# A graph network on one NeuronCore: the list scheduler's ranking of begun products, its view of the port that VectorE and GpSimd share, and the last two groups worked in halves

## The chip, the cores and the metric

The kernel runs on one core of a Trainium2 chip. The metric is the device time of one launch in microseconds, from three runs. Besides those times there is one execution taken by the hardware profiler. Engine names are those of the profile: PE is TensorE, PEld its weight loads, DVE is VectorE, ACT is ScalarE, POOL is GpSimd, SP is SyncE, which issues most of the DMAs.

## The reference, cut to what matters

The input x holds 128 graphs of 64 nodes with 256 features, all in 32-bit floats, and one 64 x 64 adjacency matrix serves all graphs. Four layers follow one another. Each normalises x over its features, takes the positive part, and adds its result to x:

```python
h = jnp.maximum(_layernorm(x, axis=-1), 0.0); x = x + _L0_gnn_ref(h, adj, ...)   # adj products, then LSTMs
h = jnp.maximum(_layernorm(x, axis=-1), 0.0); x = x + _L1_gnn_ref(h, adj, adj, ...)  # Laplacian, attention, MLP
h = jnp.maximum(_layernorm(x, axis=-1), 0.0); x = x + _L2_gnn_ref(h, adj, ...)   # graph attention
h = jnp.maximum(_layernorm(x, axis=-1), 0.0); x = x + _L3_gnn_ref(h, adj, ...)   # spectral filter
```

- Layer 0 multiplies by the adjacency and by a weight matrix, twice, and then runs four LSTMs (windows of 1, 2, 3 and 4 nodes) one after another over the result.
- Layer 1 takes a product with the scaled Laplacian, a normalisation, attention with four heads under a mask, a normalisation, a two-layer network with GELU, and a normalisation.
- Layer 2 is graph attention: two scores for each node, their sum for each pair of nodes, a leaky ReLU, a mask, a softmax over the nodes, and the product of the weights with the features and a matrix W.
- Layer 3 needs the eigenvectors U of a 64 x 64 matrix made from the adjacency. It computes `U @ (relu(U.T @ h @ W1 + b1) @ W2 + b2)`.

## The kernel before, in words

**Tiling.** Two graphs make a tile of 128 rows (partitions), so there are 64 tiles. Layer 0 is worked in 8 groups of 8 tiles. Its results are stored to DRAM, and layers 1 to 3 are worked in 16 groups of 4 tiles (`HT = 4`): a group is fetched, goes through `layer1`, `layer2` and `layer3`, and is stored two tiles at a time. A buffer of the kind "big" holds 4 tiles x 256 features. A product over the nodes of a graph (`mix`) uses 64 x 64 pieces of the PE array, four at a time. Such a series is recorded as one indivisible operation, a "burst". All other products use the whole array. In the profile every matrix product of 32-bit floats shows as two records.

**A planner writes the order.** No engine's order is written by hand. The code records every operation with `Plan.record` (line 114 on): its engine, what it depends on, the buffers that it needs. `Plan.schedule` then plays the program through on assumed costs and decides, for each engine, in which order the operations are issued and which buffer each gets. `Plan.issue` (line 341) emits them in that order, so every instruction has line 347 in the profile. [...] The assumed times decide the order alone; the chip's own durations decide when things happen.

**How the planner chooses.** For each engine it takes the operation that can start first. Among those that can start now, it takes the one with the smallest rank. Three things matter here:

- `rank` (line 331). For groups of layer 0 it sorts by group, then by the order of recording. For groups of layers 1 to 3 it sorts by group, and within that by `6 * max(op.group - g, 0) - op.path`, where `path` is the longest chain of assumed times to the program's end. The last six groups count as one group (`self.ends`), so they are run down together. Bursts are kept together by a flag ahead of the rank, since a change between 64 x 64 pieces and the whole array is charged 0.178 us. The eigenvector computation (the group `EIG`, "aside") is first on PE and GpSimd and last elsewhere.
- The port. `op.port` (line 162) marks all GpSimd operations, and VectorE operations whose operands are all in SBUF. The planner lets only one of them run at a time: after one is placed, `port = t + cost` (line 295) bars the others until its assumed end.
- PSUM. There are eight banks of 512 floats. Six are of the kind "bank" from the start. Two of the kind "seed" serve layer 0's LSTMs, and join the others when layer 0 is done. A value gets its bank when its first product is placed, and the bank comes free after its last reader.

**Costs.** `Plan.cost` (line 179) gives GpSimd `0.44 + 0.14 * n` for a power and `0.12 + 0.00218 * n` for anything else with n elements in a row. A DMA from SP is charged its transfer time and 2.2 us of latency.

**The last layers.** `ln_stats` computes means and variances of 4 tiles on VectorE, then four small GpSimd operations on 128 x 4 elements (one of them a power) make scale and shift. `relu_norm` (line 1609) applies them on ScalarE, a tile at a time. `mix_fm` (line 1616) is a burst followed by two copies out of PSUM by ScalarE. `layer2` (line 1698) and `layer3` (line 1732) work on all 4 tiles of a group in each step: every step of layer 3, for instance, waits until the step before has done all four tiles.

Of the kernel before, what the change touches and what calls it, by code (L numbers as in the profile page):

```python
# [8 lines left out]
ALU = mybir.AluOpType  # L9
# [3 lines left out]
N = 64  # L13
# [55 lines left out]
class Plan:  # L69
# [44 lines left out]
    def record(self, eng, name, args, kw):  # L114
        op = self.run
        if op is None:
            op = Op(eng, name, args, kw, self.group)
            op.lead = self.lead
            if self.behind:
                op.deps.add(self.behind)  # L120
        else:
            op.calls.append((name, args, kw))
        aps = [(a, i == 0) for i, a in enumerate(args) if self.is_ap(a)]
        aps += [(a, k in ("out", "accum_out")) for k, a in kw.items() if self.is_ap(a)]
        for a, write in aps:
            ap = a.ap if isinstance(a, Virt) else a
            if str(ap.space) == "DRAM" and not self.tc.is_my_tile(ap.tensor):
                continue
            key = ap.tensor.name
            if isinstance(a, Virt):  # L130
                key = id(a.val)
                op.vals[a.val] = True
            step, count = ap.ap[0]
            p0, f0 = (ap.offset // step, ap.offset % step) if step else (0, ap.offset)
            ends = [s * (n - 1) for s, n in ap.ap[1:]]
            region = (p0, p0 + count, f0 + sum(min(e, 0) for e in ends), f0 + sum(max(e, 0) for e in ends) + 1)
            if isinstance(a, Virt) and a.val.kind in ("bank", "seed"):
                op.deps |= {o for o in a.val.users if o.eng != eng}
                a.val.users.append(op)
            reads, writes = self.seen.setdefault(key, ([], []))  # L140
            for log in (reads, writes) if write else (writes,):
                for r, o in log:
                    if o is not op and r[0] < region[1] and region[0] < r[1] and r[2] < region[3] and region[2] < r[3]:
                        op.deps.add(o)
                        if log is writes:
                            op.late.add(o)
                if write:
                    log[:] = [(r, o) for r, o in log if not (
                        region[0] <= r[0] and r[1] <= region[1] and region[2] <= r[2] and r[3] <= region[3])]
            (writes if write else reads).append((region, op))  # L150
        if eng == "PE":

            val = args[0].val
            if val.last and val.last is not op:
                op.deps.add(val.last)
            val.last = op
        if op is self.run:
            return self.link(op)
        flat = [a.ap if isinstance(a, Virt) else a for a, _ in aps]
        op.cost, op.lat = self.cost(op, flat)  # L160

        op.port = eng == "G" or (eng == "V" and not name.startswith("bn_") and "reduce" not in name
                                 and all(str(ap.space) == "SB" for ap in flat))
        op.index = len(self.ops)
        self.ops.append(op)
        self.link(op)
        if self.whole:
            self.run = op
# [10 lines left out]
    def cost(op, aps):  # L179
# [37 lines left out]
                c += 0.12  # L217
            return c, c + 0.15
        if op.eng == "G":
            c = 0.44 + 0.14 * n if op.kw.get("op") is ALU.pow else 0.12 + 0.00218 * n  # L220
            return c, c + 0.05
        c = max(0.6, free(aps[0]) * aps[0].ap[0][1] * 4e-6 / 0.39)
        return c, c + 2.2
# [6 lines left out]
    def schedule(self):  # L230
# [20 lines left out]
        while len(order) < len(self.ops):  # L251
# [40 lines left out]
                many, cost, lat = op.many, cost + 0.178, lat + 0.178  # L292
            now[e] = t + cost
            if op.port:
                port = t + cost
            end = t + lat
            for v in op.vals:
                if v.buf is None:
# [10 lines left out]
            for o in op.after:  # L309
                o.wait -= 1  # L310
                if o.eng != e:
                    o.ready = max(o.ready, end + self.slack(o))
                else:
                    o.ready = max(o.ready, end - 0.01 if op in o.late and e != "PE" else t + cost)
                if not o.wait:
                    ready[o.eng].append(o)
# [14 lines left out]
    def rank(self, op):  # L331
        if op.group == self.aside:
            return (-2 if op.eng in ("PE", "G") else 1000, op.index)
        if op.eng == "SP":
            return (op.group, 0, op.index)
        g = min(max(op.group - op.lead, 0), self.ends)
        if op.group < REST:
            return (g, -op.lead, op.index)
        return (g, 6 * max(op.group - g, 0) - op.path, op.index)

    def issue(self):
        real = lambda a: a.real() if isinstance(a, Virt) else a
# [551 lines left out]
P = 128  # L894
# [116 lines left out]
def gnn_kernel(ctx: ExitStack, tc: tile.TileContext, a, out):  # L1011
# [54 lines left out]
    def bank(name):  # L1066
        return plan.value("bank")
# [201 lines left out]
    def tm(n=HT, f=D):  # L1269

        return plan.value("big")[:, :n * f].rearrange("p (t f) -> p t f", f=f)
# [334 lines left out]
        V.reduce_max(mx, s, axis=AX.X)  # L1606
        V.tensor_sub(s, s, mx.unsqueeze(2).to_broadcast(list(s.shape)))

    def relu_norm(x):
        sc, bi = ln_stats(x)  # L1610
        h = tm()
        for t in range(HT):
            ACT.activation(h[:, t, :], x[:, t, :], AF.Relu, scale=sc(t), bias=bi(t))
        return h

    def mix_fm(h, m):

        dst = fm()
        for i, ps in enumerate(mix(lambda t, c: h[:, t, tok(c)], m, HT)):
            evac(dst.rearrange("p c (t b n) -> p c t b n", t=HT, b=2)[:, :, :, i, :], ps, 1)  # L1620
        return dst

    def layer1(x):
# [71 lines left out]
            V.tensor_mul(x2[:, t0:t0 + 2, :], x2[:, t0:t0 + 2, :], vec(g3, 2))  # L1695
            V.tensor_add(x[:, t0:t0 + 2, :], x[:, t0:t0 + 2, :], x2[:, t0:t0 + 2, :])

    def layer2(x):


        h = relu_norm(x)
        big, stat = plan.value("big"), plan.value("stat")
        s12 = stat[:, 2 * HT:4 * HT].rearrange("p (k t) -> p k t", k=2)
        for k in range(2):
            for t in range(HT):
                V.scalar_tensor_tensor(big[:, t * D:(t + 1) * D], h[:, t, :], 1.0, wa[:, k, :], op0=ALU.mult, op1=ALU.mult, accum_out=s12[:, k, t:t + 1])

        s2d, s1m, e2, e = (big[:, i * HT * N:(i + 1) * HT * N].rearrange("p (t n) -> p t n", n=N) for i in range(4))
        V.tensor_mul(s2d, vec(ident2), s12[:, 1, :].unsqueeze(2).to_broadcast([P, HT, N]))
        G.tensor_add(s1m, vec(mask2), s12[:, 0, :].unsqueeze(2).to_broadcast([P, HT, N]))  # L1710
        ps = bank("s2")[:, :HT * N]
        PE.matmul(ps, same, flat(s2d), start=True, stop=True)
        V.tensor_add(flat(e), ps, flat(s1m))
        V.tensor_scalar(e2, e, 0.2, None, op0=ALU.mult)
        V.tensor_max(e, e, e2)
        softmax_shift(e, stat[:, :HT])
        attn = plan.value("attn").rearrange("p (t k) -> p t k", t=HT)
        for i in range(2):
            r = half(i)
            ACT.activation(attn[r, :, r], e[r], AF.Exp)  # L1720
        ssum = stat[:, HT:2 * HT]
        V.reduce_sum(ssum, attn, axis=AX.X)
        V.reciprocal(ssum, ssum)
        pT = plan.value("big")[:, :HT * P]
        evac(pT, transposes([attn[:, t, :] for t in range(HT)]), 1)
        aT = mix_fm(h, lambda t: pT[:, tok(t)])
        for t0 in (0, 2):
            ps = proj_tm(lambda c, t: aT[:, c, tok(t)], W2a, 2, t0)
            for t in (t0, t0 + 1):
                V.scalar_tensor_tensor(x[:, t, :], ps[:, (t - t0) * D:(t - t0 + 1) * D], ssum[:, t:t + 1], x[:, t, :], op0=ALU.mult, op1=ALU.add)  # L1730

    def layer3(x):
        h = relu_norm(x)
        for t0 in (0, 2):
            G.tensor_add(x[:, t0:t0 + 2, :], x[:, t0:t0 + 2, :], vec(b3b, 2))
        aT = mix_fm(h, lambda t: Ub)
        hid = tm(HT, P)
        ps = bank("hid")
        for t in range(HT):
            for c in range(2):  # L1740
                PE.matmul(ps[:, tok(t)], aT[:, c, tok(t)], W3a[:, c, :], start=c == 0, stop=c == 1)
        V.tensor_tensor(hid, ps.rearrange("p (t f) -> p t f", t=HT), vec(nb3a), op=ALU.max)
        uT = tm(HT, P)
        for i, ps in enumerate(mix(lambda t, c: hid[:, t, :], lambda t: UTb, HT, 1)):
            V.tensor_tensor(uT.rearrange("p t (b n) -> p t b n", b=2)[:, :, i, :], ps[:, 0], vec(C3[:, half(i)]), op=ALU.add)
        for t0 in (0, 2):
            ps = proj_tm(lambda c, t: uT[:, t, :], W3b.unsqueeze(1), 1, t0)
            V.tensor_add(pair(x, t0), ps, pair(x, t0))

    for g in range(NT // HT):  # L1750
        plan.group = REST + g
        x = fetch(put[g // 2][:, g % 2 * HT:(g % 2 + 1) * HT])
        layer1(x)
        layer2(x)
        layer3(x)
        for t0 in range(0, HT, 2):
            SP.dma_start(xout[g][:, t0:t0 + 2, :], x[:, t0:t0 + 2, :])
    plan.issue()
# [53 lines left out]
```

## Time and profile before

| | |
|---|---|
| runs, median (lowest to highest) | 2116.32 us (2113.99 to 2117.18) |
| the profiled execution's own time | 2117.02 us |
| its span, first to last instruction | 2115.2 us |
| instructions | 48093 |
| PE, DVE, ACT, POOL busy | 2072.3, 1767.0, 1094.7, 756.6 us |
| groups of layer 0 and the eigenvectors | about 0 to 1270 us |
| groups of layers 1 to 3 | about 1270 us to the end |

The profile is read from whole to part: the busy time of each engine over the span; then the same by stretches of time, which shows where PE, the busiest, is idle; then PE's waits and the chain of waits in the stretch where it is idle most; then single instructions there. A line of such a view names the engine, the operation, what it writes and reads (buffer numbers left out, so `big<-bank,Whh` is a buffer of the kind big, written from a PSUM bank and from a constant that lives in the memory once used for Whh), the shape as partitions x elements, and how many were merged.

### The profile page before, as it was taken

The numbers are of one execution on the slowest core, as the hardware profiler recorded it, in microseconds if no ns is written. First come the engines' busy times: TensorE is split into PE (matmuls) and PEld (weight loads), VectorE is DVE, ScalarE is ACT, GpSimd is POOL, SyncE is SP. The second block draws the span as 40 slices with busy tenths as digits, with TensorE's granted clock in tenths as the row PEclk, the third lists the DMA queues.
The fourth block names the chain that finished last, engine by engine and source line by source line (L and its number), as shares of the span: only waits on it lengthen the run. The fifth ranks groups of instructions, "written<-read, shape, count | busy, mean of one in ns | idle before, by whom it ended". The sixth has DMA issues, their size and how long they took to land.

```text
span 2115.2 us, 48093 instructions
## 1 busy us (share of the span) xinstructions
PE 2072.3 (98%) x17924; PEld 1675.9 (79%) x17924; DVE 1767.0 (84%) x6669; ACT 1094.7 (52%) x2451; POOL 756.6 (36%) x1144
## 2 busy tenths in 40 slices
PE   8999999999999999999999999999999999999997
PEld 6688689688788788788788789877778778877775
DVE  7788888889999999999988956868779699885785
ACT  3344544534543543543444345666666567575763
POOL 6522212222201201201100215685467658663452
PEclk9999999999999999999999999999999999999999
DMA  6000100100100100100000211100000000000001
GB/s 229 1 3 13 52 3 2 62 2 2 60 1 1 61 1 2 46 1 10 32 1 21 90 49 35 62 1 22 22 21 22 21 22 22 22 2 11 1 12 51
DMA packets 44875, 57.83 MB, mean 27 GB/s; under 512 B 8929, under 2 KB 38497, under 8 KB 44641
## 3 DMA queue, kind: packets, MB, share of 16 engines
q1 hardware_dynamic: 43536, 53.71, 7.9%
q8 instruction: 141, 2.31, 0.5%
q10 hardware_dynamic: 1104, 1.05, 0.2%
q14 instruction: 94, 0.76, 0.1%
HBM read 37.53 MB, written 16.78 MB: 26 GB/s over the span
## 4 chain that ended last, share of the span: by engine, by line
PE 80%; DVE 13%; issue 2%; ACT 2%; POOL 2%; DMA 0%; SPq 0%; ACTq 0%; DVEq 0%; POOLq 0%
PE bank L347 64%; PE seed L347 16%; DVE arena L347 5%; DVE big L347 4%; DVE stat L347 2%; ACT mids L347 1%; DVE mids L347 1%; POOL stat L347 1%; DVE sums L347 1%; POOL big L347 1%; ACT big L347 0%; DMA arena<-put 0%; DVE bank L347 0%; POOL sums L347 0%; DVE seed L347 0%
## 5 line engine op out<-in xcount | busy, mean ns | idle before, releaser
L347 PE MATMUL bank<-big,Wih 128*128 128x512 f32 (+4 forms) x1802 | 554.5, 424 | 2.9 <-DVE big L347 1.9
L347 PEld LDWEIGHTS bank<-big,Wih 128*128 128x128 f32 x1802 | 314.7, 190 | 145.5 <-issue 95.5
L347 PE MATMUL bank<-big,sums 128*128 128x128 f32 (+3 forms) x2328 | 375.7, 289 | 5.2 <-DVE seed L347 2.5
L347 ACT ACTIVATE mids<-bank,bl 128x512 f32<-128x512 f32 (+2 forms) x432 | 247.2, 576 | 214.3 <-PE bank L347 195.2
L347 PEld LDWEIGHTS bank<-big,sums 128*128 128x128 f32 (+1 forms) x2328 | 298.5, 180 | 42.8 <-issue 19.6
L347 PE MATMUL bank<-big,Whh 128*128 128x128 f32 (+3 forms) x1294 | 312.3, 327 | 0.0
L347 DVE TENSOR_TENSOR arena<-arena 64x42 f32<-64x42 f32 (+6 forms) x1358 | 276.5, 231 | 18.4 <-POOL arena L347 1.2
L347 PEld LDWEIGHTS bank<-big,Whh 128*128 128x128 f32 x1294 | 214.0, 191 | 18.5 <-issue 10.5
L347 ACT ACTIVATE mids<-seed,bl 128x256 f32<-128x256 f32 (+2 forms) x192 | 102.0, 531 | 217.0 <-PE seed L347 209.0
L347 DVE TENSOR_TENSOR big<-mids 128x512 f32<-128x512 f32 (+2 forms) x256 | 151.1, 597 | 27.1 <-ACT mids L347 17.1
L347 POOL TENSOR_SCALAR stat<-stat 128x4 f32<-128x4 f32 (+1 forms) x228 | 68.4, 301 | 281.1 <-DVE stat L347 268.9
L347 PE MATMUL seed<-big,sums 128*128 128x128 f32 (+3 forms) x896 | 143.3, 291 | 0.0
L347 DVE SCALAR_TENSOR_TENSOR arena<-arena 64x1 f32<-64x1 f32 (+15 forms) x565 | 136.1, 264 | 4.5 <-POOL arena L347 1.0
L347 POOL TENSOR_TENSOR big<-big 128x128 f32<-128x128 f32 (+2 forms) x55 | 32.9, 600 | 294.6 <-DVE big L347 151.7
L347 POOL TENSOR_TENSOR stat<-stat,mhalf 128x4 f32<-128x4 f32 (+1 forms) x114 | 123.9, 1087 | 4.8
L347 ACT COPY seed<-bank 128x128 f32<-128x128 f32 (+2 forms) x192 | 54.0, 281 | 135.8 <-PE bank L347 128.5
L347 ACT ACTIVATE mids<-big 128x256 f32<-128x256 f32 (+2 forms) x176 | 89.5, 511 | 66.3 <-DVE big L347 62.1
L347 ACT COPY mids<-bank 128x256 f32<-128x256 f32 (+3 forms) x290 | 94.8, 352 | 51.9 <-PE bank L347 51.5
L347 PEld LDWEIGHTS seed<-big,sums 128*128 128x128 f32 (+1 forms) x896 | 118.4, 183 | 3.5 <-issue 0.3
L347 DVE TENSOR_SCALAR arena<-arena 64x1 f32<-64x1 f32 (+10 forms) x506 | 100.4, 206 | 7.8 <-POOL arena L347 0.5
L347 DVE TENSOR_TENSOR big<-big,mids 128x256 f32<-128x256 f32 (+2 forms) x196 | 99.0, 509 | 7.0 <-ACT mids L347 6.0
L347 PE MATMUL bank<-Wih,big 128*128 128x256 f32 x408 | 104.8, 383 | 0.0
(517 smaller groups left out, 4480.4 us busy)
## 6 DMA issues: line engine op xcount, KB each, us to landing
big<-in_x_dram SPq DMA_DIRECT2D x29, 512.0 KB, 5.0
put<-big SPq DMA_DIRECT2D x15, 512.0 KB, 3.2
big<-put SPq DMA_DIRECT2D x8, 512.0 KB, 6.4
out_dram<-big SPq DMA_DIRECT2D x16, 256.0 KB, 2.6
Wih<-in_WihT_dram SPq DMA_DIRECT2D x3, 1024.0 KB, 11.4
Whh<-in_WhhT_dram SPq DMA_DIRECT2D x3, 1024.0 KB, 12.9
arena<-put SPq DMA_DIRECT2D x3, 512.0 KB, 5.9
sums<-put SPq DMA_DIRECT2D x3, 512.0 KB, 4.3
```

The costliest lines, as they stand in the source:

```text
L347: getattr(self.engines[op.eng], name)(*map(real, args), **{k: real(a) for k, a in kw.items()})
```

## The change

Six edits. Five are in the planner, and change no operation, only the order and the choice of buffers:

1. `begun(op)` is true for a PE operation one of whose PSUM values already has its bank. In groups of layer 0 such an operation gets group 0 in its rank, so it comes ahead of operations of all groups that have not begun a bank. In groups of layers 1 to 3 it gains 6 us of path.
2. `op.hold`: an operation all of whose operands have two dimensions and at most 64 elements in a row bars the port for at most 0.06 us instead of its whole cost. This holds for GpSimd and for VectorE.
3. A GpSimd operation other than a power, with at most 64 elements, is charged 0.2 us (for 4 elements it was 0.129).
4. What depends on a DMA from SP and runs on another engine is taken to be ready 1.5 us later than before.
5. For this, `relu_norm` and `mix_fm` take a range of tiles.

The sixth changes operations: `layer2` and `layer3` take a `step`. It is 4 tiles for groups 0 to 13, and 2 tiles for the last two groups. Every step of both layers, with its statistics, softmax, bursts and copies, is then recorded once for tiles 0 and 1 and once for tiles 2 and 3, and neither half waits for the other. The diff, cut:

```diff
@@ record
+        wide = max(ap.ap[-1][1] if len(ap.ap) == 2 else 65 for ap in flat) > 64
+        op.hold = op.cost if wide else 0.06
@@ cost
-            c = 0.44 + 0.14 * n if op.kw.get("op") is ALU.pow else 0.12 + 0.00218 * n
+            c = 0.44 + 0.14 * n if op.kw.get("op") is ALU.pow else 0.12 + 0.00218 * n if n > 64 else 0.2
@@ schedule
             if op.port:
-                port = t + cost
+                port = t + min(cost, op.hold)
...
                 if o.eng != e:
-                    o.ready = max(o.ready, end + self.slack(o))
+                    o.ready = max(o.ready, end + self.slack(o) + (1.5 if e == "SP" else 0.0))
@@ rank
         if op.group < REST:
-            return (g, -op.lead, op.index)
-        return (g, 6 * max(op.group - g, 0) - op.path, op.index)
+            return (0 if self.begun(op) else g, -op.lead, op.index)
+        return (g, 6 * max(op.group - g, 0) - op.path - (6 if self.begun(op) else 0.0), op.index)
+
+    def begun(self, op):
+
+        return op.eng == "PE" and any(v.kind in ("bank", "seed") and v.buf is not None for v in op.vals)
@@ helpers
-    def relu_norm(x):
-        sc, bi = ln_stats(x)
-        h = tm()
-        for t in range(HT):
-            ACT.activation(h[:, t, :], x[:, t, :], AF.Relu, scale=sc(t), bias=bi(t))
+    def relu_norm(x, h=None, t0=0, n=HT):
+        h = tm() if h is None else h
+        sc, bi = ln_stats(x[:, t0:t0 + n], n)
+        for t in range(n):
+            ACT.activation(h[:, t0 + t, :], x[:, t0 + t, :], AF.Relu, scale=sc(t), bias=bi(t))
         return h
-    def mix_fm(h, m):
-
-        dst = fm()
-        for i, ps in enumerate(mix(lambda t, c: h[:, t, tok(c)], m, HT)):
-            evac(dst.rearrange("p c (t b n) -> p c t b n", t=HT, b=2)[:, :, :, i, :], ps, 1)
+    def mix_fm(h, m, dst=None, t0=0, n=HT):
+
+        dst = fm() if dst is None else dst
+        part = dst[:, :, t0 * P:(t0 + n) * P].rearrange("p c (t b n) -> p c t b n", t=n, b=2)
+        for i, ps in enumerate(mix(lambda t, c: h[:, t0 + t, tok(c)], lambda t: m(t0 + t), n)):
+            evac(part[:, :, :, i, :], ps, 1)
         return dst
@@ layers 2 and 3
+    def layer2(x, step):
+
+        h, big, attn = tm(), plan.value("big"), plan.value("attn").rearrange("p (t k) -> p t k", t=HT)
+        pT, aT = plan.value("big")[:, :HT * P], fm()
+        for t0 in range(0, HT, step):
+            n, ts = step, slice(t0, t0 + step)
+            relu_norm(x, h, t0, n)
+            stat = plan.value("stat")
...
+            mix_fm(h, lambda t: pT[:, tok(t)], aT, t0, n)
...
+    def layer3(x, step):
+        h, aT, hid, uT = tm(), fm(), tm(HT, P), tm(HT, P)
+        for t0 in range(0, HT, step):
+            n, ts = step, slice(t0, t0 + step)
+            relu_norm(x, h, t0, n)
+            for u0 in range(t0, t0 + n, 2):
+                G.tensor_add(x[:, u0:u0 + 2, :], x[:, u0:u0 + 2, :], vec(b3b, 2))
+            mix_fm(h, lambda t: Ub, aT, t0, n)
...
+            V.tensor_tensor(hid[:, ts], ps[:, :n * P].rearrange("p (t f) -> p t f", t=n), vec(nb3a, n), op=ALU.max)
+            for i, ps in enumerate(mix(lambda t, c: hid[:, t0 + t, :], lambda t: UTb, n, 1)):
+                V.tensor_tensor(uT[:, ts].rearrange("p t (b n) -> p t b n", b=2)[:, :, i, :], ps[:, 0], vec(C3[:, half(i)], n), op=ALU.add)
+            for u0 in range(t0, t0 + n, 2):
+                ps = proj_tm(lambda c, t: uT[:, t, :], W3b.unsqueeze(1), 1, u0)
+                V.tensor_add(pair(x, u0), ps, pair(x, u0))
...
         layer1(x)
-        layer2(x)
-        layer3(x)
+        step = 2 if g >= NT // HT - 2 else HT
+        layer2(x, step)
+        layer3(x, step)
```

More of the change, by code (lines that the diff above doesn't have):

```diff
@@ L1696, in layer1 @@
             V.tensor_add(x[:, t0:t0 + 2, :], x[:, t0:t0 + 2, :], x2[:, t0:t0 + 2, :])
[L1698 to L1748, printed above, removed]
+    def layer2(x, step):
[5 more added lines that the diff above has]
+            stat = plan.value("stat")
+            s12 = stat[:, 2 * HT:2 * HT + 2 * n].rearrange("p (k t) -> p k t", k=2)
+            for k in range(2):
+                for t in range(n):
+                    V.scalar_tensor_tensor(big[:, (t0 + t) * D:(t0 + t + 1) * D], h[:, t0 + t, :], 1.0, wa[:, k, :], op0=ALU.mult, op1=ALU.mult, accum_out=s12[:, k, t:t + 1])
+            s2d, s1m, e2, e = (big[:, (t0 * 4 + i * n) * N:(t0 * 4 + (i + 1) * n) * N].rearrange("p (t n) -> p t n", n=N) for i in range(4))
+            V.tensor_mul(s2d, vec(ident2, n), s12[:, 1, :].unsqueeze(2).to_broadcast([P, n, N]))
+            G.tensor_add(s1m, vec(mask2, n), s12[:, 0, :].unsqueeze(2).to_broadcast([P, n, N]))
+            ps = bank("s2")[:, :n * N]
+            PE.matmul(ps, same, flat(s2d), start=True, stop=True)
+            V.tensor_add(flat(e), ps, flat(s1m))
+            V.tensor_scalar(e2, e, 0.2, None, op0=ALU.mult)
+            V.tensor_max(e, e, e2)
+            softmax_shift(e, stat[:, :n])
+            for i in range(2):
+                r = half(i)
+                ACT.activation(attn[r, ts, r], e[r], AF.Exp)
+            ssum = stat[:, HT:HT + n]
+            V.reduce_sum(ssum, attn[:, ts], axis=AX.X)
+            V.reciprocal(ssum, ssum)
+            pt = bank("tr")
+            for t in range(n):
+                PE.transpose(pt[:, tok(t)], attn[:, t0 + t, :], ident)
+            evac(pT[:, t0 * P:(t0 + n) * P], pt[:, :n * P], 1)
+            mix_fm(h, lambda t: pT[:, tok(t)], aT, t0, n)
+            for u0 in range(t0, t0 + n, 2):
+                ps = proj_tm(lambda c, t: aT[:, c, tok(t)], W2a, 2, u0)
+                for t in (u0, u0 + 1):
+                    V.scalar_tensor_tensor(x[:, t, :], ps[:, (t - u0) * D:(t - u0 + 1) * D], ssum[:, t - t0:t - t0 + 1], x[:, t, :], op0=ALU.mult, op1=ALU.add)
@@ new lines, in layer3 @@
+    def layer3(x, step):
[6 more added lines that the diff above has]
+            mix_fm(h, lambda t: Ub, aT, t0, n)
+            ps = bank("hid")
+            for t in range(n):
+                for c in range(2):
+                    PE.matmul(ps[:, tok(t)], aT[:, c, tok(t0 + t)], W3a[:, c, :], start=c == 0, stop=c == 1)
+            V.tensor_tensor(hid[:, ts], ps[:, :n * P].rearrange("p (t f) -> p t f", t=n), vec(nb3a, n), op=ALU.max)
+            for i, ps in enumerate(mix(lambda t, c: hid[:, t0 + t, :], lambda t: UTb, n, 1)):
+                V.tensor_tensor(uT[:, ts].rearrange("p t (b n) -> p t b n", b=2)[:, :, i, :], ps[:, 0], vec(C3[:, half(i)], n), op=ALU.add)
+            for u0 in range(t0, t0 + n, 2):
+                ps = proj_tm(lambda c, t: uT[:, t, :], W3b.unsqueeze(1), 1, u0)
+                V.tensor_add(pair(x, u0), ps, pair(x, u0))
```

## The prediction

> **What bounds the kernel now.** First the page's busy times, then the same by stretches: start, LSTMs, change-over with the end of the eigenvectors, layers 1 to 3, and the last 74 us.
>
> ```profile
> PE 2072.3 (98%) x17924; PEld 1675.9 (79%) x17924; DVE 1767.0 (84%) x6669; ACT 1094.7 (52%) x2451; POOL 756.6 (36%) x1144
> ...
> 0.00:60.00 60.00, 54.25 (x618) 38.09 (x619) 47.03 (x183) 20.68 (x48) 43.00 (x71) 0.94 0.59 202
> 60.00:1130.00 1070.00, 1066.09 (x7345) 860.80 (x7344) 960.03 (x4203) 486.23 (x1245) 200.26 (x363) 1.00 0.06 18
> 1130.00:1330.00 200.00, 194.52 (x1438) 170.97 (x1438) 144.95 (x530) 94.00 (x230) 52.88 (x86) 1.00 0.16 49
> 1330.00:2041.00 711.00, 701.78 (x7552) 559.57 (x7551) 563.15 (x1592) 462.56 (x871) 433.96 (x585) 1.00 0.06 19
> 2041.00:2115.20 74.20, 55.68 (x980) 46.47 (x978) 51.87 (x164) 31.20 (x60) 26.54 (x40) 0.95 0.13 44
> ```
>
> After each stretch's length come PE, PEld, DVE, ACT and POOL busy. PE sets the pace: it idles 5.8 us in the start, 3.9 + 5.5 + 9.2 = 18.6 us from 60 to 2041, and 18.5 us in the last 74 us. No PE work is removed, so a better order can win no more than these 43 us and what hides in busy time. The last stretch, by finer windows (same columns), changes its limit half-way:
>
> ```profile
> 2041.00:2073.00 32.00, 26.36 (x518) 22.53 (x517) 31.41 (x112) 19.47 (x37) 13.78 (x23) 1.00 0.06 19
> 2073.00:2085.00 12.00, 9.59 (x216) 8.21 (x218) 10.38 (x29) 6.52 (x13) 8.43 (x12) 1.00 0.27 89
> 2085.00:2095.00 10.00, 8.21 (x102) 7.16 (x92) 4.07 (x10) 2.05 (x4) 0.16 (x1) 1.00 0.17 54
> ```
>
> Up to 2085 DVE works 41.8 of 44 us: it is the limit. After that nothing is full; one group's chain of steps sets the end. The timeline shows that chain, the last group's layer 3 (the last number in a row is the wait before it):
>
> ```profile
> 2093.80 1.39 DVE L347 BATCH_NORM_STATS2 stat<-big 128x6 f32<-128x256 f32 x4
> 2095.87 1.04 POOL L347 TENSOR_TENSOR stat<-stat,mhalf 128x4 f32<-128x4 f32 x1
> 2097.53 2.07 ACT L347 ACTIVATE sums<-big,stat 128x256 f32<-128x256 f32 x4 [10.44 <-POOL stat L347]
> 2102.45 0.59 ACT L347 COPY sums<-seed 128x512 f32<-128x512 f32 x1 [2.84 <-PE bank L347]
> 2103.57 2.05 PE L347 MATMUL bank<-Whh,sums 128*128 128x128 f32 x16 [1.17 <-ACT sums L347]
> 2105.66 0.69 DVE L347 TENSOR_TENSOR big<-bank,Whh 128x512 f32<-128x512 f32 x1 [3.79 <-PE bank L347]
> 2107.95 0.81 PE L347 MATMUL seed<-Wih,big 128*128 128x256 f32 x2 [0.84 <-DVE big L347]
> 2111.42 0.69 DVE L347 TENSOR_TENSOR big<-bank,big 128x512 f32<-128x512 f32 x1 [0.16 <-PE bank L347]
> ```
>
> Each engine works alone and then waits. From the first statistics to the last addition this takes 2112.1 - 2093.8 = 18.3 us, and the last store lands 3.1 us later. Near 2098 to 2101.6 and 2108.4 to 2111.8 a product of 256 columns takes 0.85 us rather than 0.43: PE's clock was halved.
>
> **What the Trainium skill says.** "SBUF — State Buffer", section "Who interferes with whom": VectorE with two SBUF inputs contends with a GpSimd instruction that reads SBUF. The trace agrees for large operations and not for small. Setting DVE's rows of the timeline against POOL's, an SBUF-to-SBUF 128x256 tensor operation takes 414 ns alone (227 cases), 654 ns under a large POOL operation (48), 412 ns under a small one (29). So the planner's bar was wrong for the small ones and the edit describes the chip better. "TensorEngine Tiling (Array Packing)", "Key Properties": changing the tiling mode drains TensorE. The trace agrees: 19 bursts from 60 to 1130 us cost 0.095 us on entry and 0.13 on leaving beyond the records' own pace, 0.23 us each. "TensorE: Matmul & The Clock Gate", "What's actually happening": after an idle window of about 3.4 us the clock is halved; the two slow stretches above, 3.4 us each, agree.
>
> **The change part by part.** The sum is made against the profiled execution's 2117.02 us (2115.2 of span and 1.8 around it), 0.7 above the median of the runs.
>
> *Halves, the gain.* Each step of the last group's layer 3 is halved; the second half ends last. Its chain: statistics 2 x 0.33 and aggregation 0.2: 0.86. Small POOL operations: the power on 128x2 takes 0.712 (four such in group 0) rather than 1.04, with three others and gaps 1.5. Two activations 1.1. Half a burst with its latency and release 0.8. Two copies of 128x256 at 0.375 (row of such copies), 0.75, and release 0.2. W3a half of 2.05, 1.03, latency 0.3. Maximum on 128x256 0.41. Second burst with releases 0.9. Two additions of 128x128 at 0.28, 0.56, release 0.2. Two products at 0.85, 1.7, latency 0.3. Addition 0.69. Sum 11.3, so 7.0 us less, if the first half is out of the way; none at all if the first half's steps simply push the second's. I take -7.0, because no engine is half full after 2085. In layer 2 of the last group, after its exponentials (2082.7) up to 2093.8, half the transposes, copies, W2a products and additions is worth 3.5 us by the same rows, but PE works on the other groups there (8.2 of 10 us); I take half, -1.7. The stores keep their number and queue; the first two tiles' may go earlier, and the last still takes 3.1 us.
>
> *Halves, the cost.* DVE per group: in layer 2, five operations of 128x256 become ten of 128x128 (0.41 to 2 x 0.28: 0.15 each), scale, row sum and reciprocal add 0.1 + 0.13 + 0.13; in layer 3 the maximum adds 0.14 and the additions 0.3. That is 1.55, for two groups 3.1 us, and DVE is the limit up to 2085: on the path, +3.1. ACT 1.2 per group (copies 0.59 to 2 x 0.375, exponentials 0.41 to two of about 0.3), 2.3 in all, beside DVE (ACT 26.0 of 44 us busy). POOL: the power 1.04 to 2 x 0.71, three more small ones of 0.2, twice per group, and the mask's addition: 4.3 in all, hidden by POOL's own idle time (22.2 of 44 us busy), save where ACT waits, which the chain above counts. PE: three more bursts a group, 6 x 0.23 = 1.4, hidden by PE's idle 8 us before 2085; without that cover 1.4 us on the end. No wait is added that holds other work, but each half has its own semaphore at the head of a queue: a late first half on ACT would hold back the other group's copies behind it, and these W3a.
>
> *The planner's edits.* No instruction changes up to about 2000 us. What the new costs and ranks can change is the order, and so the 18.6 us of idle PE from 60 to 2041 and the mode changes (132 recorded bursts run in 90 series here: up to 42 x 0.23 = 9.7 us if all come apart, and a gain if more meet). For a gain: the small POOL operations, six times 1.4 us of plan time a group in layers 1 to 3, no longer bar VectorE in the plan; a bank begun is finished and evacuated sooner. Against: PE waits in many small pieces (none over 2 us), for DVE and ACT results, with no sign that PSUM is what lacks; any new order draws new waits. Bound: -9 to +9. I take -2.5. The later readiness behind DMAs: DVE waits only 1.6 us for a fetch after 1230, and stretches of the start are 5.8 us idle; bound -2 to +2, taken as 0. The 0.2 us cost: same bound as the order's, not counted again.
>
> Sum: -7.0 - 1.7 + 3.1 - 2.5 = -8.1 us. From 2117.0 that is 2108.9; from the median 2108.2. I state **2108.5 us**. About 0.2% (4.2 us) is what a measurement of this kernel can tell from no change.
>
> **Rivals.**
>
> *The halves bring nothing.* The chain after 2085 only moves: the first half's activations, copies and products stand in the queues before the second's, and DVE's 3.1 us are added to a full engine. For it: ACT alone has 2.07 + 1.18 us a group in this layer, PE about 6. Against: between these steps every engine idles (10.4 us before the activations). It would give -7.0 - 1.7 back: 2116.3 + 3.1 - 2.5 = 2116.9, no change.
>
> *The order of the body becomes much better.* True costs let DVE's and ACT's results arrive as planned; idle PE from 60 to 2041 falls from 18.6 to 8 us. For it: the 412 ns above. Against: the remaining idle pieces are each near 0.3 to 1 us, about one release. It gives 2116.3 - 5.6 - 10.6 = 2100.
>
> *A worse order in the body, slower.* A begun product of a younger layer-0 group now goes ahead of the older group's unbegun gates (group 0 against its own), and 6 us of path do the like later. The older group's recurrence, PE to ACT to DVE and back, stretches; PE lives from younger work as long as there is some, then idles at the change-over (1130 to 1330, where PE already waits 1.0 and 1.1 us for DVE) and in layers 1 to 3. Price: one us per us of idle PE. Against: PE takes only what is ready, and it has had spare work nearly always. It decides when idle PE (or mode changes) beyond 60 us grows by more than 5.6 + 4.2 = 9.8 us, i.e. from 18.6 to above 28; with 13 more, 2124.
>
> **How the numbers follow.** Forecast 0.53 (its own range 2102 to 2112); better order 0.14 (below 2102); halves bring nothing 0.15 (2112 to 2120); worse order 0.18 (above 2120.5). Faster: 0.53 + 0.14 = 0.67; same 0.15; slower 0.18. The range: 2097 to 2122 leaves out 0.04 below, the far end of the better order, and 0.15 above, most of the worse order.
>
> **What would show it.** Right: the last group's layer 3 from first statistics to last addition takes 10 to 14 us, with POOL powers on 128x2 of 0.71; DVE's busy time grows by about 3 us, POOL's by 4; idle PE after the place where DVE fills up falls from 18.5 to about 12; idle PE from 60 to 2041 stays within 10 to 28. Wrong: the chain at the end still spans 17 us or more (second rival), or the idle time of the body leaves that band (third and fourth). The forecast fails above all if re-ordering moves more than halving does, which no view of this profile can exclude.

## The result, and the profile after

The changed kernel takes 2103.53 us (median of four runs, 2102.98 to 2105.87), the kernel before 2116.32 us. The ratio is 0.9941, with a 95% interval of 0.9926 to 0.9956: 12.8 us less. The forecast was 8 us less, and all four runs lie in the stated range, near the faster end of the forecast's own case (2102 to 2112).

The page of the profiled execution (2102.98 us, span 2101.2) and the same stretches as before; columns again PE, PEld, DVE, ACT and POOL busy:

```profile
PE 2066.1 (98%) x17928; PEld 1677.7 (80%) x17928; DVE 1766.8 (84%) x6691; ACT 1095.6 (52%) x2465; POOL 774.0 (37%) x1162
...
0.00:60.00 60.00, 52.88 (x614) 37.49 (x615) 44.29 (x172) 20.03 (x44) 48.05 (x73) 0.94 0.59 202
60.00:1130.00 1070.00, 1062.73 (x7319) 858.89 (x7318) 964.81 (x4243) 485.51 (x1245) 200.54 (x361) 1.00 0.06 18
1130.00:1330.00 200.00, 194.68 (x1491) 171.40 (x1490) 140.91 (x507) 94.93 (x228) 49.07 (x82) 1.00 0.16 51
1330.00:2041.00 711.00, 703.06 (x7674) 564.92 (x7673) 568.33 (x1601) 467.31 (x884) 448.30 (x594) 1.00 0.06 19
2041.00:2101.20 60.20, 52.70 (x838) 45.05 (x836) 48.48 (x173) 27.83 (x65) 28.01 (x54) 0.99 0.17 54
```

PE's idle time before 2041 is 7.1 us in the start (before: 5.8) and 7.3 + 5.3 + 7.9 = 20.5 us from 60 to 2041 (before: 18.6). So no idle time was won there. After 2041 it is 7.5 us instead of 18.5. The finer windows of that stretch:

```profile
2041.00:2073.00 32.00, 30.86 (x464) 27.26 (x462) 31.45 (x118) 17.56 (x38) 16.81 (x33) 1.00 0.12 40
2073.00:2085.00 12.00, 11.15 (x217) 9.17 (x206) 9.65 (x35) 6.79 (x20) 7.06 (x14) 1.00 0.22 70
2085.00:2095.00 10.00, 9.30 (x166) 7.81 (x168) 5.61 (x18) 3.48 (x8) 4.14 (x7) 1.00 0.20 64
```

DVE is as full as before in the first 32 us (31.45 against 31.41), but PE now works 30.86 us of them instead of 26.36. The last group's layer 3, second half, from the timeline:

```profile
2087.10 0.74 DVE L353 BATCH_NORM_STATS2 stat<-big 128x6 f32<-128x256 f32 x2
2088.71 0.71 POOL L353 TENSOR_TENSOR stat<-stat,mhalf 128x2 f32<-128x2 f32 x1
2090.05 1.09 ACT L353 ACTIVATE mids<-big,stat 128x256 f32<-128x256 f32 x2 [1.59 <-POOL stat L353]
2092.16 0.65 ACT L353 COPY sums<-seed 128x256 f32<-128x256 f32 x2 [1.01 <-PE seed L353]
2092.85 1.16 PE L353 MATMUL bank<-Whh,sums 128*128 128x128 f32 x8 [0.50 <-ACT sums L353]
2094.05 0.42 DVE L353 TENSOR_TENSOR sums<-bank,Whh 128x256 f32<-128x256 f32 x1 [1.17 <-PE bank L353]
2096.13 1.13 PE L353 MATMUL seed<-Wih,big 128*128 128x256 f32 x4 [0.86 <-DVE big L353]
2097.40 0.69 DVE L353 TENSOR_TENSOR big<-seed,big 128x512 f32<-128x512 f32 x1 [1.32 <-PE seed L353]
```

From 2087.1 to 2098.1 this half takes 11.0 us. Before, the whole group took 18.3. The half also begins 6.7 us earlier than the whole group did (2087.1 against 2093.8). 7.3 + 6.7 is the 14.0 us between the two spans.

To place differences, the sections below use one more quantity, PE's *lost time*: from each PE record's start to the next one's start, less the usual pace of its shape (the lower quartile in the kernel before, such as 216 ns for 256 columns; 14.5 ns for a record of a burst), summed over a stretch. Unlike idle time it also counts short waits and a slow clock. It adds up to the differences between the spans within 1 us. In this table e1 is the kernel before with the halves alone, e2 the changed kernel without the halves; more on both below.

| lost PE time, us | 0 to 1330 | 1330 to 1797 | from 1797 | sum |
|---|---|---|---|---|
| before | 51.5 | 25.2 | 30.5 | 107.2 |
| after | 54.7 | 21.6 | 17.1 | 93.4 |
| e1, halves alone | 53.5 | 24.4 | 26.1 | 104.0 |
| e2, planner's edits alone | 56.5 | 21.9 | 21.4 | 99.8 |

The cut at 1797 us is there because the halves leave all earlier work in its old order: VectorE's sequence in e1 first departs from that of the kernel before at 1797.6 us, and after's first departs from e2's at 1796.6 us. Two executions of the same order differ by some 2 us in the first column (before and e1, after and e2).

A part of the last column is the clock. In the kernel before it was halved for 3.4 us twice before the last product ended, at 2098.2 and 2108.4 us:

```profile
2094.80:2098.20 3.40, 1.19 (x34) 1.03 (x35) 2.00 (x9) 0.67 (x2) 1.69 (x4) 0.99 0.00 0
2098.20:2101.60 3.40, 3.40 (x30) 2.28 (x32) 1.11 (x2) 1.41 (x3) 2.49 (x2) 0.50 0.00 0
2105.00:2108.40 3.40, 1.77 (x40) 1.42 (x39) 1.45 (x3) 0.00 (x0) 0.00 (x0) 1.00 0.00 1
2108.40:2111.80 3.40, 2.91 (x8) 1.75 (x6) 1.07 (x2) 0.00 (x0) 0.00 (x0) 0.50 0.00 0
```

PE was busy for 3.40 + 2.91 us of the two; half of that, an estimate of 3.2 us, is lost to the clock. In the kernel after it was halved only from 2099.8 us on, when the last product (2097.3) was done, so nothing is lost. These are single executions.

### The profile page after: what moved, and what is told of

It reads as the page before. It is cut to its first block, busy times and chain, and to the rows that moved or that the text cites. A ratio compares the mean times of both kernels' runs of the same rounds, so it can differ in the third digit from the quotient of the medians.

```text
span 2101.2 us, 48168 instructions
## 1 busy us (share of the span) xinstructions
PE 2066.1 (98%) x17928; PEld 1677.7 (80%) x17928; DVE 1766.8 (84%) x6691; ACT 1095.6 (52%) x2465; POOL 774.0 (37%) x1162
## 4 chain that ended last, share of the span: by engine, by line
PE 81%; DVE 13%; ACT 2%; issue 1%; POOL 1%; DMA 0%; ACTq 0%; DVEq 0%
PE bank L353 65%; PE seed L353 16%; DVE big L353 5%; DVE arena L353 4%; DVE stat L353 2%; DVE mids L353 1%; ACT mids L353 1%; DVE sums L353 1%; POOL stat L353 1%; ACT sums L353 0%; ACT big L353 0%; POOL big L353 0%; DMA big<-in_x_dram 0%; DVE seed L353 0%; POOL sums L353 0%
## 5 line engine op out<-in xcount | busy, mean ns | idle before, releaser
L353 PE MATMUL bank<-big,sums 128*128 128x128 f32 (+3 forms) x1968 | 362.4, 300 | 4.0 <-DVE seed L353 2.4
L353 PE MATMUL bank<-big,Whh 128*128 128x128 f32 (+4 forms) x1416 | 328.4, 327 | 0.3 <-ACT sums L353 0.3
L353 PEld LDWEIGHTS bank<-big,sums 128*128 128x128 f32 (+1 forms) x1968 | 287.3, 187 | 42.2 <-issue 20.9
L353 DVE TENSOR_TENSOR arena<-arena 64x42 f32<-64x42 f32 (+6 forms) x1359 | 272.2, 228 | 18.4 <-POOL arena L353 0.6
L353 PEld LDWEIGHTS bank<-big,Whh 128*128 128x128 f32 (+1 forms) x1416 | 220.7, 187 | 31.1 <-issue 20.3
L353 DVE SCALAR_TENSOR_TENSOR arena<-arena 64x1 f32<-64x1 f32 (+16 forms) x565 | 131.1, 255 | 8.6 <-POOL arena L353 3.0
L353 ACT ACTIVATE mids<-big 128x512 f32<-128x512 f32 (+2 forms) x176 | 89.1, 511 | 80.3 <-DVE big L353 75.9
L353 POOL TENSOR_TENSOR big<-big,B1T 128x512 f32<-128x512 f32 x32 | 36.4, 1138 | 206.3 <-DVE big L353 154.1
L353 PE MATMUL seed<-big,Whh 128*128 128x128 f32 (+4 forms) x476 | 111.4, 326 | 0.0
L353 DVE TENSOR_SCALAR arena<-arena 64x1 f32<-64x1 f32 (+9 forms) x507 | 102.1, 211 | 7.4 <-POOL arena L353 0.3
L353 POOL MEMSET arena<- 64x2 f32 (+5 forms) x72 | 7.8, 113 | 261.9 <-DVE arena L353 261.7
## 6 DMA issues: line engine op xcount, KB each, us to landing
Wih<-in_WihT_dram SPq DMA_DIRECT2D x3, 1024.0 KB, 12.6
```

The lines of the kernel that those rows point to most:

```text
L353: getattr(self.engines[op.eng], name)(*map(real, args), **{k: real(a) for k, a in kw.items()})
```

## Experiments

Three theories were put to them: A, that the halves make the gain and the planner's edits little; B, that the planner's new order makes it; C, that any new order of this program moves the time by as much. After e1 and e2, A means that each edit has its own worth, and B that the port edit is what makes the order good.

### Halves alone, planner alone

e1 takes the planner's four edits out of the kernel after (the fifth in the list of the change only prepares two helpers for the halves); e2 takes the halves out:

```diff
# e1
-                port = t + min(cost, op.hold)
+                port = t + cost
-        ... 0.12 + 0.00218 * n if n > 64 else 0.2
+        ... 0.12 + 0.00218 * n
-        o.ready = max(o.ready, end + self.slack(o) + (1.5 if e == "SP" else 0.0))
+        o.ready = max(o.ready, end + self.slack(o))
-            return (0 if self.begun(op) else g, -op.lead, op.index)
-        return (g, 6 * max(op.group - g, 0) - op.path - (6 if self.begun(op) else 0.0), op.index)
+            return (g, -op.lead, op.index)
+        return (g, 6 * max(op.group - g, 0) - op.path, op.index)
# e2
-        step = 2 if g >= NT // HT - 2 else HT
+        step = HT
```

> Before, with layers 2 and 3 of the last two groups in halves and none of the planner's edits. Theory A, the halves make the gain: 8 to 13 us below the kernel before, and the last group's layer 3 (from the second half's first statistics to the last addition) in about 11 us. Theory B, the planner's new order makes it: within 3 us of before or slower, since the halves add 3.1 us of VectorE work where VectorE is full. Theory C, any new order moves the time by that much: anything from 10 us below to 10 above.

> After, with whole groups of four tiles everywhere: the planner's four edits alone. Theory A: within 4 us of the kernel before, idle PE after 2041 us still about 18 us. Theory B: 8 to 13 us below before, with idle PE after 2041 us down to about 8 us. Theory C: anything within 10 us either way.

e1: 2113.84 us, ratio 0.9987 (0.9980 to 0.9993). e2: 2109.95 us, ratio 0.9965 (0.9951 to 0.9978). Beside 2116.72 for the kernel before on the same chip this is -2.9 and -6.8 us. Neither is the whole; together they make 9.7 of 12.8. So A and B both fall as the only cause, though e1 alone lies just within what B allowed; C had room for both. The timeline of e2 at its end shows what the halves lack there, a last group in whole steps:

```profile
2086.16 0.74 DVE L353 BATCH_NORM_STATS2 stat<-big 128x6 f32<-128x256 f32 x2
...
2093.43 1.53 DVE L353 TENSOR_TENSOR sums<-bank,sums 128x512 f32<-128x512 f32 x2 [1.32 <-PE bank L353]
2098.50 0.69 DVE L353 TENSOR_TENSOR mids<-seed,Whh 128x512 f32<-128x512 f32 x1 [3.54 <-PE seed L353]
...
2103.89 0.69 DVE L353 TENSOR_TENSOR big<-bank,big 128x512 f32<-128x512 f32 x1 [1.01 <-PE bank L353]
```

In e2 the last group's layer 3 takes 2104.6 - 2086.2 = 18.4 us, as before the change; but it begins 7.6 us earlier than the 2093.8 of the kernel before. So the kernel with the planner's edits comes sooner to the last group's layer 3, and the halves shorten that layer. In e1 the second half begins at 2096.4, 2.6 us later than the kernel before, and takes 12.6 us.

### A nudge that means nothing

e3 changes the kernel before, and e4 the kernel after, in one assumed cost, the charge for a change between 64 x 64 pieces and the whole array; e11 moves it the other way:

```diff
-                many, cost, lat = op.many, cost + 0.178, lat + 0.178
+                many, cost, lat = op.many, cost + 0.185, lat + 0.185    # e3 (before), e4 (after); e11 (before): 0.171
```

> Before, with the planner's charge for a change of the array's tiling 0.185 us instead of 0.178: a change that describes nothing better, only draws another order. Theories A and B: within 3 us of before. Theory C: 5 us or more away from before, to either side.

> After, with the same nudge from 0.178 to 0.185 us. Theories A and B: within 3 us of the kernel after, so about 10 to 16 us below before. Theory C: 5 us or more away from the kernel after, to either side.

> Before, with the planner's charge for a change of tiling 0.171 us instead of 0.178. If the 20 us of the first nudge were a rare draw: within 5 us of before. If orders under the old port scatter widely: 8 us or more away, to either side.

e3: 2136.88 us, ratio 1.0092 (1.0079 to 1.0106). e11: 2117.53 us, ratio 1.0001 (0.9992 to 1.0009). e4: 2102.58 us, ratio 0.9928 (0.9916 to 0.9941). A change of 7 ns in an assumed cost made the kernel before 20 us slower, more than the whole change won; the same step the other way changed nothing that can be measured. That is theory C's outcome for one of three. The windows show where e3 loses most (columns as above):

```profile
1330.00:1797.00 467.00, 450.69 (x4968) 366.62 (x4967) 367.72 (x1031) 296.76 (x573) 294.52 (x396) 0.99 0.08 24
```

The same stretch of the kernel before:

```profile
1330.00:1797.00 467.00, 458.39 (x5182) 370.50 (x5181) 381.12 (x1077) 302.89 (x586) 305.07 (x411) 1.00 0.08 24
```

PE idles 16.3 us there in e3, 8.6 in the kernel before. The lost time says 39.0 against 25.2. PE's waits in e3 from 1330 to 2041 us (total, times, longest) name no single cause; the three largest:

```profile
PE bank L347 <- issue: 3.3, 3, 1.6
PE bank L347 <- DVE sums L347: 3.2, 2, 2.3
PE bank L347 <- ACT mids L347: 3.1, 1, 3.1
...
```

In three parts of this stretch the clock was halved in e3's profiled execution:

```profile
1367.10:1370.50 3.40, 3.05 (x12) 2.78 (x13) 3.40 (x10) 2.79 (x6) 3.32 (x4) 0.50 0.00 0
1612.90:1619.70 6.80, 6.02 (x51) 5.02 (x51) 6.66 (x25) 1.76 (x4) 3.08 (x5) 0.50 0.00 0
1626.50:1629.90 3.40, 3.40 (x10) 2.65 (x9) 3.40 (x16) 1.39 (x3) 2.92 (x4) 0.50 0.00 0
```

Half of PE's busy time in them is 6.2 us, an estimate of what the clock cost: nearly half of the 13.8 us of lost time that e3 has more in this stretch. The rest is waits of the new order. The clock was not so slow in all of e3's runs: one with a mean clock of 0.996 took 2132.7 us, the three with 0.992 to 0.993 took 2136.5 to 2139.2. Even the first is 16 us slower than the kernel before. So what the planner's edits won is not settled by one comparison: it is a draw beside other draws.

### One edit of the planner at a time

Each takes one edit out of the kernel after. e8 keeps the rank for begun products in layers 1 to 3 only.

```diff
# e5: no rank for begun products
-            return (0 if self.begun(op) else g, -op.lead, op.index)
-        return (g, 6 * max(op.group - g, 0) - op.path - (6 if self.begun(op) else 0.0), op.index)
+            return (g, -op.lead, op.index)
+        return (g, 6 * max(op.group - g, 0) - op.path, op.index)
# e6: the old port
-                port = t + min(cost, op.hold)
+                port = t + cost
-        ... 0.12 + 0.00218 * n if n > 64 else 0.2
+        ... 0.12 + 0.00218 * n
# e7: DMA consumers as before
-        ... end + self.slack(o) + (1.5 if e == "SP" else 0.0))
+        ... end + self.slack(o))
# e8: begun products only from layer 1 on
-            return (0 if self.begun(op) else g, -op.lead, op.index)
+            return (g, -op.lead, op.index)
```

> After, without the rank for begun products, both in layer 0 and in layers 1 to 3. Theory A (halves and a better order, each edit with its own worth): 3 to 6 us slower than the kernel after. Theory B (the port is what makes the order good): within 2 us of after. Theory C (the order is luck): anything from 5 below to 20 us above after.

> After, with the old port (an operation bars it for its whole cost) and the old GpSimd cost. Theory A: 3 to 6 us slower than after, and the loss lies in layers 1 to 3, where the small GpSimd operations are. Theory B: about 7 us slower, that is all of what the planner's edits alone brought. Theory C: anything from 5 below to 20 us above after.

> After, without the 1.5 us on what depends on a DMA from SP. Theories A and B: within 2 us of after. Theory C: anything from 5 below to 20 us above after. If the 3 us that PE loses more than before in the first 1330 us come from this edit, they are back here.

> After, with the rank for begun products in layers 1 to 3 alone, and layer 0 ranked as before. If that rank in layer 0 is what costs the 3 us that PE loses more than before in the first 1330 us, this is about 3 us faster than after (2100). If those come from the DMA edit or from the port, it is within 1 us of after. Theory C: anything from 5 below to 20 us above.

| kernel | median, us | ratio to before (95%) |
|---|---|---|
| e5, no begun rank | 2102.28 | 0.9935 (0.9917 to 0.9953) |
| e6, old port | 2114.34 | 0.9993 (0.9985 to 1.0002) |
| e7, no DMA edit | 2101.04 | 0.9931 (0.9912 to 0.9950) |
| e8, begun rank from layer 1 on | 2103.31 | 0.9943 (0.9922 to 0.9965) |

Without the rank for begun products, and without the DMA edit, the kernel is as fast as after: neither brings a gain that shows. Without the port edit no gain can be told from zero (the interval of e6 holds 1). But the loss isn't where the small GpSimd operations are, which was expected: in the lost time e6 has 61.9, 19.3 and 23.4 us (after: 54.7, 21.6, 17.1). It loses 7 us before 1330 us and 6 after 1797, and gains 2 between. The 3 us that PE loses more than before in the first 1330 us, which e7 and e8 were to place, are not placed: e5, e7 and e8 have about 55, 55 and 53 us there, no further from after's 54.7 than two executions of one order are.

### The port edit by itself

e9 is the kernel after with the e5 and e7 edits both, so that of the planner's edits only the port's is left; e10 is e9 without the halves.

> Before, with the halves and the port edit (hold and the small GpSimd cost), without the rank for begun products and without the 1.5 us behind DMAs. If these two edits are the whole of the change's worth: 2099 to 2104. If the edits need one another, 2108 or more.

> Before, with the port edit alone. If the port edit is what the planner's edits brought: 2106 to 2111, and with e9 about 8 us below it, as after is below e2. If the port edit only makes up for what the ranks and the DMA edit cost in layer 0: 2113 to 2118, like before.

e9: 2112.86 us, ratio 0.9986 (0.9979 to 0.9992). e10: 2120.57 us, ratio 1.0014 (1.0007 to 1.0021). e9 is in the second of its ranges and e10 above both of its own: the port edit is not enough, though e6 made it look like the cause. The port edit with either one of the others gives 2101 to 2104 us; it alone, or the other two without it, gives 2113 to 2114 (all with halves). So the edits don't add up, and since a nudge of 7 ns can do what e6 did and more, these runs can't say which of them *makes* the order good.

Where e9 and e10 lose is known: before 1330 us their lost time is about 61 and 60 us, 8 us more than in e1 and in the kernel before (53.5 and 51.5); about 1.7 us of e9's are a halved clock. Why they lose it there is open. One candidate is a wait of PE for the arena, which holds the eigenvector computation: its small products are first in rank on PE, and PE stands at one until VectorE delivers its operand. PE's waits from 60 to 1330 us (who waits for whom; total, times, longest), first the kernel before:

```profile
PE bank L347 <- DVE arena L347: 1.9, 3, 1.1
```

The kernel after:

```profile
PE bank L353 <- DVE arena L353: 4.6, 7, 1.6
```

And e10:

```profile
PE bank L353 <- DVE arena L353: 4.6, 8, 2.0
```

These waits are 2.7 us longer in after and in e10. But they do not follow the port edit. In e6, which lacks it, they are longest; in e7, which has it, they are as short as before:

```profile
PE bank L353 <- DVE arena L353: 6.4, 11, 1.2
PE bank L353 <- DVE arena L353: 2.0, 8, 0.4
```

So it is not shown that the port edit makes them.

Three pairs now show the halves over a fixed order of the rest: e1 against before -2.9 us, e9 against e10 -7.7, after against e2 -6.4 (the last pair was not run on the same chip). Each pair has one order of VectorE until about 1797 us; after that the order differs too, so the spread from 2.9 to 7.7 is that of the draw as well.

### Four groups in halves

```diff
-        step = 2 if g >= NT // HT - 2 else HT
+        step = 2 if g >= NT // HT - 4 else HT
```

> After, with the last four groups in halves instead of two. If shorter steps help wherever groups run out: 2 to 5 us faster than after. If only the end of the last group counts and the rest costs VectorE 1.55 us a group where it is full: 1 to 4 us slower.

e12: 2102.90 us, ratio 0.9935 (0.9919 to 0.9952): the same as after. Two more groups in halves neither help nor cost, against both expectations. Of all kernels run, none is faster than after by more than the intervals.

## Why the prediction was right, and where not

**The halves, in layer 3** (-7.0): right. With everything before 1797 us in the same order, e2's 18.4 us became 11.0, so -7.4; the sum had 11.3 for the second half. The near match hides two misses: the last two products and their latency took 1.3 us and not 2.0, since the clock was not halved there as the sum assumed, and the other steps took 0.4 us more. In the other two pairs it is 18.3 to 12.6 (e1) and 16.9 to 10.8 (e9). In all nine kernels with halves the second half takes 10.8 to 12.6 us. The sum has no term for the halved clock by itself. In the kernel before that was about 3.2 us, in e2 about 1.1, in after and e1 nothing, so it is a part of what both the halves and the new order won in these executions; in the pair of e9 and e10 it went the other way (3.1 and 1.7 us). The prediction also read the two slow stretches as agreeing with a clock that is halved after an idle window of 3.4 us. Their length agrees, but PE had not been idle: it was busy for 1.2 and 1.8 of the 3.4 us ahead of them.

**The halves, before that** (-1.7 + 3.1 = +1.4): right in sign, and in size within some 1 us. The last statistics begin 0.9 us later in after than in e2, 2.6 later in e1 than before, 0.5 later in e9 than in e10. The two terms are not shown apart. In e1 DVE's busy time grew by 3.0 us (1767.0 to 1770.0), but 1.8 of these lie before 1797 us, where nothing was changed; in the other two pairs it fell (e2 1773.6 to after 1766.8, e10 1763.7 to e9 1759.9).

**The planner's edits** (-2.5, bound -9 to +9): the size is what was off. They brought -6.8 us as e2, 4.3 more than was taken, and this is nearly all of the 4.7 us by which the sum fell short of 12.8. The step that failed was the confinement: the prediction let a new order change only the idle time from 60 to 2041 us, and kept the last 74 us for the halves. There it was the other way: idle PE from 60 to 2041 was 18.6 us before, 19.1 in e2 and 20.5 in after, while e2's lost time after 1797 us fell from 30.5 to 21.4. The stretch from 2041 us to the last group's first statistics of layer 3 (in after, those of its second half) shows what changed, for before, e2 and after:

```profile
2041.00:2093.80 52.80, 44.02 (x820) 37.90 (x818) 44.66 (x147) 28.05 (x54) 22.36 (x34) 1.00 0.13 42
2041.00:2086.16 45.16, 40.32 (x795) 33.88 (x794) 39.87 (x133) 26.54 (x52) 21.57 (x32) 1.00 0.13 43
2041.00:2087.10 46.10, 44.11 (x681) 38.26 (x679) 41.90 (x155) 25.45 (x59) 24.74 (x49) 1.00 0.15 48
```

Of the 7.6 us by which it is shorter in e2, 4.8 are VectorE work that is no longer in it and 2.8 idle time of VectorE; of the 6.7 in after, 2.8 and 3.9. PE idles 8.8, 4.8 and 2.0 us. So the new order both left VectorE less to do at the end and kept PE fed beside a VectorE that was as full: in the first 32 us DVE works 31.4 us in all three, PE 26.4, 28.7 and 30.9. That VectorE was the limit there is therefore not refuted, only that PE had to wait as much for it. Changes of the array's tiling, which the prediction also counted, gave little: the bursts run in 84 series in e2 and 87 in after instead of 90, which at the measured 0.23 us is 1.4 and 0.7 us.

That the total fell into the stated range is in part luck. The -2.5 was picked within a bound and not summed from steps, and one meaningless nudge of the same planner moved the time by 20 us (e3).

**The rivals.** "The halves bring nothing" fell. "The order of the body becomes much better" did not come: idle PE from 60 to 2041 is 20.5 us and not 8, and what the order won lies after it. "A worse order" did not come in this draw, but its fear did in e3: more than the price named (+20 us against +13), and mostly in layers 1 to 3. Its mechanism, begun products of younger groups that go ahead, is not what costs there: e3 has no such rank, and e5 and e8, which take it out of after (e8 in layer 0 only), change nothing that can be measured.

**The marks.** POOL powers on 128x2 of 0.71: yes. PE idle after 2041 of about 12: 7.5 in after, since the new order won there too; e1, with the halves alone, has 71.1 - 59.6 = 11.5. Last group's layer 3 in 10 to 14 us "from first statistics": 16.6 from the first half's, 11.0 from the second half's, which is what the sum was about; the mark was worded for the wrong half. POOL's busy time +4: it rose by 17.4, of which 15.5 are in e2 and so come from the order. DVE's +3: after has 0.2 less than before, and e2, without the halves, has 6.6 more; so the 3 us do not show above what orders and executions do.

**What stays open.** Whether the planner's edits describe the chip better and therefore order better, or drew well. For the first: the five kernels with halves, the port edit and at least one other (after, e4, e5, e7, e8) all lie between 2101 and 2104 us, though VectorE's sequence in e4, e5, e7 and e8 departs from after's at 12.6, 122.8, 2.1 and 2.1 us; e12, with four groups in halves, is at 2102.9. Against it: e9 and e10. More nudges of each would tell; they weren't run. Nor does a run check the port edit for small VectorE operations: the 412 ns of the prediction are large VectorE operations beside small GpSimd ones.

## What to carry to other kernels

Where a program ends in one chain of short steps on different engines, cut the last work in two and sum the second half's chain step by step; such a sum of 11.3 us came within 1.3 us of all nine second halves here, in part because misses cancelled. Before crediting an edit of a scheduler's costs, nudge a cost that means nothing: here that alone moved the time by 20 us, so a gain of 7 us from such an edit, true or drawn, can't be told by one build. An engine that is full is no proof that the others must wait for it as much as they do: ask also how much of its work another order could do earlier, and what else could run beside it.

## What the runs showed that was not expected

- A full VectorE with PE at 96%: 31.45 and 30.86 of the same 32 us (after), where the same DVE load left PE at 82% before and at 90% in e2.
- 7 ns in one assumed cost gave +20.2 us (e3), and 7 ns the other way +0.5 us (e11).
- PE's clock is halved without PE being idle. In the fourteen profiles, after the first 20 us, PE was busy for up to 1.8 of the 3.4 us ahead of each halving. So short waits close together can cost twice: 6.2 of the 13.8 us that e3 loses more than before between 1330 and 1797 us are an estimate of the slow clock alone.
